# Row sums of four heads in one pass of the array, with their quotients spread through DRAM

## The chip, the cores and the metric

The kernel runs on one core of one Trainium2 chip. The metric is the time of one execution on the device in microseconds (us); lower is better. Runs of this kernel agree within about 0.02%: the three shown below lie between 2488.17 and 2488.77 us. The core has five engines that work side by side, each in its own order: TensorE (PE, with its weight loads PEld), VectorE (DVE), ScalarE (ACT), GpSimd (POOL) and SyncE (SP), which issues all DMA transfers here. Matmuls write to PSUM, the other engines read it; everything else lies in SBUF or in DRAM.

## The reference

Four layers work on x of shape (4, 512, 32, 32): four batches of 512 channels and 1024 tokens, all in fp32. Layers 0 and 3 are softmax attentions, layer 1 a linear attention, layer 2 a softmax attention with one head. The part that the change touches, from layer 0:

```python
attn = jnp.einsum('bihd,bjhd->bijh', q, k) * SCALE
attn = jax.nn.softmax(attn, axis=2)
res = jnp.einsum('bijh,bjhd->bihd', attn, v)
...
out = res @ Wo.T + bo + xs
```

Layer 0 has 8 heads of 64 channels, layer 3 has 4 heads of 128 and a group norm ahead of its projections. Softmax divides the exponentials of a row by their sum; the kernel divides after the product with v, which gives the same.

## The kernel before

The program has two paths. `plain_path` computes everything without subtracting the row's largest score and counts at the end whether all row sums and their reciprocals stayed below 1e18; `general_path` would run afterwards if they had not. With these inputs only `plain_path` runs, and only it is changed.

**Order.** TensorE runs its instructions in the order in which the program is written. The order on the other engines is settled when the kernel is built; each engine then executes its own list in order. Tiles come from pools with tags: a tag has so many buffers, and a new tile of the tag waits until the last reader of the old one is done.

**Layers.** Layer 0 goes over the four batches: projections of q, k and v for a batch, then its attention. While the projections of batch b run, layer 1 (linear attention) of batch b-1 is done piece by piece. Layer 2 follows for four batches (`one_head`), then layer 3. Large products use a seven-product scheme on 2x2 blocks, which is not touched.

**Attention of layers 0 and 3** (`attention`, L892). A unit is a query block `qb` (two of 512 queries) and a group `g` of 128 channels: four units to a query block, eight to a batch. In layer 0 a unit is a pair of heads of 64 (`pair`), in layer 3 one head of 128. Scores are computed with keys on the partitions and queries along the free axis. A step covers 128 keys in layer 0 (8 steps to a unit) and 256 in layer 3 (4 steps).

- `scores` (L908): the score products (L913 for pairs, in 64x64 quadrants of the array, or L918), the exponential on ACT into a tile `pt` (L922, four buffers), and on DVE the sum over steps into `acc` (L926, L929; tag `sum`, two buffers). In layer 3 the two halves of `acc` are added at the end (L931).
- `values` (L933): products of `pt` with v (L941 or L956) into PSUM accumulators of the tag `acc` (four buffers), two steps behind the scores. A pair uses two accumulators, added into the tile `ot` at the end of the unit (L951 on ACT, L952 on DVE). In layer 3 the one accumulator stays until the unit is normalised.
- `sum_rows` (L961): the sum over the partitions by a matmul with a matrix of ones, so that each of the 128 result rows holds the same row sum of its head. For a pair these are four quadrant products into two accumulators (L968), which ACT and DVE add (L973, L974); in layer 3 one full product (L976). `invert` (L673) then takes the reciprocal on DVE (L675, which is in the tile `rd`) and two DVE reductions, the largest sum and the largest reciprocal, for the range check (L677, L678).
- `normalise` (L980): `ot` times `rd` on DVE (L985), and on ACT the bias of the output projection added to x (L988).
- `project_out` (L996): the output projection of a query block in four parts, each of 256-column products (L1018) and DVE additions (L1026), the last ones into x. The first part needs groups 0 and 1 of `ot`, the second groups 2 and 3.

**Ticks.** Work that must wait is put in the list `later` with a number. Each step of values calls `tick` (L648), which counts all numbers down and runs what has come to zero. In layer 0 a unit's `sum_rows` and `normalise` come at tick 1 after it, in layer 3 the sum comes just ahead of the unit's last values. The four parts of `project_out` come at ticks 4, 5, 6, 7 after a query block in layer 0 and 2, 3, 3, 4 in layer 3.

**x.** A batch of x is 2 MB, 16 KB on each partition. The tag `x` has three buffers. `away` (L568) writes a batch to DRAM, `back` (L572) reads it again; both are issued by SP. In layer 2, while batch b is worked on, the layer norm of batch b+1 is prepared (`layer_norm`, L1466), and at the end of a batch it goes away and another one comes back.

Of the kernel before, what the change touches and what calls it, by code (L numbers as in the profile page):

```python
# [13 lines left out]
F32 = mybir.dt.float32  # L14
AF = mybir.ActivationFunctionType
ALU = mybir.AluOpType
AX = mybir.AxisListType

P = 128
# [455 lines left out]
def plain_path(ctx: ExitStack, tc: tile.TileContext, d: dict, out: bass.AP, count):  # L475
# [9 lines left out]


    nc = tc.nc
# [23 lines left out]
    def sum_tile(name):  # L511
        return work.tile([P, 2, TB], F32, tag="sum", bufs=2, name=name)

    def v_tiles():
# [49 lines left out]
    def x_tile(b):  # L564
        xs[b] = xpool.tile([P, NC, S], F32, tag="x", bufs=B - 1, name=f"x{b}")
        return xs[b]
# [24 lines left out]
    wo0 = load_wo(d["wo0"])  # L591
    for b in range(1, B - 1):
        nc.sync.dma_start(x_tile(b), xin[b])

# [22 lines left out]
    UNITS = B * NTB * (NC + 1 + NC)  # L617
    tops = const.tile([P, 2, UNITS], F32, name="tops")
    unit = itertools.count()

# [52 lines left out]
    def invert(rd, ps):  # L673

        nc.vector.reciprocal(rd, ps)  # L675
        n = next(unit)
        nc.vector.tensor_reduce(tops[:, 0, n : n + 1], ps, AX.X, ALU.max)  # L677
        closing[:] = [nc.vector.tensor_reduce(tops[:, 1, n : n + 1], rd, AX.X, ALU.max).ins]  # L678

# [212 lines left out]
    def attention(b, q, key, v, heads, scale, wo, os, bo, hooks={}, last=False, end=None, plain=False):  # L892
# [13 lines left out]
        half = lambda i: slice(i * P // 2, (i + 1) * P // 2)  # L906

        def scores(n):  # L908
            qb, g, i = steps[n]
# [12 lines left out]
            exps.append(nc.scalar.activation(pt, ps, AF.Exp, scale=scale).ins)  # L922
            pts[n] = pt
            if i == 1:
                accs[qb, g] = acc = sum_tile("sum")
                nc.vector.tensor_tensor(acc, pts[n - 1], pt, ALU.add)  # L926
            elif i > 1:
                acc = accs[qb, g]
                nc.vector.tensor_tensor(acc, acc, pt, ALU.add)  # L929
            if i == nsteps - 1 and not pair:  # L930
                nc.vector.tensor_tensor(acc[:, 0, :], acc[:, 0, :], acc[:, 1, :], ALU.add)  # L931

        def values(n):  # L933
# [20 lines left out]
            for s in range(2):  # L954
                j = 2 * i + s
                nc.tensor.matmul(  # L956
                    outs[qb, g][0], lhsT=v[j // 2][:, j % 2, bass.ts(g, P)], rhs=pt[:, s, :],
                    start=(j == 0), stop=(j == NT - 1),
                )

        def sum_rows(qb, g):  # L961
# [16 lines left out]
            invert(rds[qb, g], ps)  # L978

        def normalise(qb, g):  # L980
            rd = rds.pop((qb, g))
            if g == 0 and not pair:
                ots[qb] = chunks_tile("ot", "ot")
            o = ots[qb][:, g, :]
            nc.vector.tensor_tensor(o, o if pair else outs.pop((qb, g))[0], rd, ALU.mult)  # L985
            xv = x[:, g, bass.ts(qb, TB)]
            with tc.issue_after(exps[-1]):
                nc.scalar.activation(xv, xv, AF.Identity, bias=bo[:, g : g + 1])  # L988
# [108 lines left out]
        for m in range(0, len(steps) + 2, per):  # L1097
# [3 lines left out]
            for n in range(m, m + per):  # L1101
                if n >= 2:
                    qb, g, i = steps[n - 2]
                    final = i == nsteps - 1

                    if final and not pair:
                        sum_rows(qb, g)
                    values(n - 2)
                    tick()
                    if final and pair:  # L1110
                        later.append([1, lambda qb=qb, g=g: (sum_rows(qb, g), normalise(qb, g))])
                    elif final:
                        normalise(qb, g)
# [5 lines left out]
                    elif final and g == NC - 1:  # L1119
                        rest = []  # L1120
                        later.append(
                            [2 * per, lambda qb=qb, rest=rest: rest.extend(project_out(qb))]
                        )
                        for i in (1, 2, 3) if pair else (1, 1, 2):
                            later.append([2 * per + i, lambda rest=rest: rest.pop(0)()])
                if parts:
# [339 lines left out]
    def layer_norm(b, tb, tiles):  # L1466

        x = xs[b][:, :, bass.ts(tb, TB)]
        t = {}

        def add():
            s = t["s"] = row_tile("s")
            nc.vector.tensor_tensor(s, x[:, 0, :], x[:, 1, :], ALU.add)
            for c in range(2, NC):
                nc.vector.tensor_tensor(s, s, x[:, c, :], ALU.add)

        def center():
# [4 lines left out]
            for c in range(NC):  # L1482
                nc.vector.scalar_tensor_tensor(
                    xn[:, c, :], mean, -1.0 / C, x[:, c, :], ALU.mult, ALU.add
                )
# [76 lines left out]
    def verdict():  # L1562

        assert next(unit) == UNITS
        ok = const.tile([P, 2 * UNITS], F32, name="ok")
# [8 lines left out]
    with tc.manual_schedule(engines={mybir.EngineType.PE}):  # L1574
# [8 lines left out]
        for b in range(B):  # L1583
# [9 lines left out]
            if b > 0:  # L1593
                away(b - 1)
                if b == 1:
                    nc.sync.dma_start(x_tile(B - 1), xin[B - 1])
                else:
                    back(b - 2)
            if b == 0:
# [70 lines left out]
        for b in range(B):  # L1670
# [25 lines left out]
            if b == 0:  # L1696
                pieces.append(lambda: (away(B - 1), back(2)))
            parts = []
# [31 lines left out]
            away(b)  # L1730
            back((b + 3) % B)
            if b + 1 < B:
# [11 lines left out]
        for b in range(B):  # L1744
# [10 lines left out]
            flush()  # L1755
            if b == 1:
                xs.pop(0)
                back(B - 1)
            hooks = {}
# [77 lines left out]
```

## Time and profile before

| What | Value |
|---|---|
| Median of three runs | 2488.47 us (2488.17 to 2488.77) |
| The profiled execution | 2487.56 us |
| Its span, first to last instruction | 2485.8 us, 24942 instructions |
| Granted TensorE clock | 0.999 |
| Attention of layer 0, one batch (326.0 to 453.9) | 127.9 us, PE busy 126.95 |
| Attention of layer 3, one batch (1909.5 to 2038.8) | 129.3 us, PE busy 129.3 |
| Reciprocals L675 | 32 in layer 0, 3352 ns each; 32 in layer 3, 3357 ns each; 8 in layer 2 |
| Range reductions L677, L678 | 628 to 672 ns each |
| Exponentials L922 | 384, 1022 ns each |
| A batch of x to DRAM and back | 6.3 us and 7.8 us from issue to landing |

The profile is that of one execution. A line of a group reads: line of the kernel, engine, operation, what it writes and reads, shapes, number; then busy time in us, mean duration in ns; then the engine's idle time just before such instructions and what ended it. A line of the timeline starts with start and duration in us. `64*64` is the part of the array that a matmul uses, rows by columns. A matmul instruction in fp32 leaves two records, and the records of successive matmuls overlap, so that a busy TensorE is not yet a TensorE at its peak. The time from issue to landing of a DMA ends when all of it has arrived.

### The profile page before, as it was taken

The numbers are of one execution on the slowest core, as the hardware profiler recorded it, in microseconds if no ns is written. First come the engines' busy times: TensorE is split into PE (matmuls) and PEld (weight loads), VectorE is DVE, ScalarE is ACT, GpSimd is POOL, SyncE is SP. The second block draws the span as 40 slices with busy tenths as digits, with TensorE's granted clock in tenths as the row PEclk, the third lists the DMA queues.
The fourth block names the chain that finished last, engine by engine and source line by source line (L and its number), as shares of the span: only waits on it lengthen the run. The fifth ranks groups of instructions, "written<-read, shape, count | busy, mean of one in ns | idle before, by whom it ended". The sixth has DMA issues, their size and how long they took to land.

```text
span 2485.8 us, 24942 instructions
## 1 busy us (share of the span) xinstructions
PE 2468.6 (99%) x10218; PEld 1277.3 (51%) x10218; DVE 1679.0 (68%) x1941; ACT 705.0 (28%) x863; POOL 253.6 (10%) x240
## 2 busy tenths in 40 slices
PE   9999999999999999999999999999999999999999
PEld 4545544554455444544645546445556446555653
DVE  3788588858875888647486775755664773665465
ACT  1454154315531544221211201112211320321121
POOL 4001100110011001201203021021010001002000
PEclk9999999999999999999999999999999999999999
DMA  5000010001000301010101010110010000000000
GB/s 216 1 1 1 5 69 1 1 5 69 1 1 5 119 10 51 0 72 9 59 0 68 5 67 19 51 68 17 17 51 1 5 13 17 1 17 17 1 9 27
DMA packets 23304, 72.47 MB, mean 29 GB/s; under 512 B 1808, under 2 KB 9488, under 8 KB 21136
## 3 DMA queue, kind: packets, MB, share of 16 engines
q1 hardware_dynamic: 23184, 70.82, 7.8%
q8 instruction: 82, 1.34, 0.2%
q14 instruction: 38, 0.31, 0.0%
HBM read 44.60 MB, written 25.17 MB: 28 GB/s over the span
## 4 chain that ended last, share of the span: by engine, by line
PE 96%; DVE 3%; issue 1%; ACT 0%; DMA 0%; SPq 0%; DVEq 0%
PE acc L703 20%; PE acc L824 11%; PE sc L918 9%; PE acc L956 9%; PE sc L913 8%; PE acc L941 8%; PE acc L831 8%; PE acc L1018 6%; PE acc L1232 6%; PE acc L1193 2%; PE acc L968 1%; PE acc L976 1%; PE feat L638 1%; DVE sum L929 1%; PE acc L638 1%; DVE rd L675 1%
## 5 line engine op out<-in xcount | busy, mean ns | idle before, releaser
L922 ACT ACTIVATE pt<-sc 128x1024 f32<-128x1024 f32 x384 | 380.3, 1022 | 650.4 <-PE sc L918 391.5
L929 DVE TENSOR_TENSOR sum<-sum,pt 128x1024 f32<-128x1024 f32 x256 | 313.9, 1226 | 45.8 <-ACT pt L922 34.4
L941 PE MATMUL acc<-pt,v 64*64 64x512 f32 x2048 | 291.0, 590 | 0.0
L913 PE MATMUL sc<-q,k 64*64 64x512 f32 x2048 | 273.7, 591 | 1.1 <-ACT pt L922 1.1
L956 PE MATMUL acc<-pt,v 128*128 128x512 f32 x512 | 239.9, 592 | 0.0
L918 PE MATMUL sc<-q,k 128*128 128x512 f32 x512 | 239.8, 593 | 0.0
L675 DVE RECIPROCAL rd<-acc 128x512 f32<-128x512 f32 x32 | 107.4, 3357 | 107.0 <-PE acc L976 107.0
L691 POOL TENSOR_TENSOR ws<-wqkv 128x256 f32<-128x256 f32 (+1 forms) x40 | 40.6, 1015 | 1334.8 <-PE acc L968 552.3
L703 PE MATMUL acc<-t,ws 128*128 128x512 f32 x384 | 173.9, 593 | 0.0
L941 PEld LDWEIGHTS acc<-pt,v 64*64 64x64 f32 x2048 | 104.2, 133 | 121.3 <-issue 98.3
L913 PEld LDWEIGHTS sc<-q,k 64*64 64x64 f32 x2048 | 101.1, 133 | 123.6 <-issue 92.4
L956 PEld LDWEIGHTS acc<-pt,v 128*128 128x128 f32 x512 | 97.3, 190 | 122.5 <-issue 120.5
L918 PEld LDWEIGHTS sc<-q,k 128*128 128x128 f32 x512 | 96.8, 190 | 112.8 <-issue 88.1
L703 PEld LDWEIGHTS acc<-t,ws 128*128 128x128 f32 x384 | 72.5, 190 | 86.6 <-issue 85.1
L675 DVE RECIPROCAL rd<-rs 128x512 f32<-128x512 f32 x32 | 107.3, 3352 | 1.1
L926 DVE TENSOR_TENSOR sum<-pt 128x1024 f32<-128x1024 f32 x64 | 76.7, 1198 | 42.1 <-ACT pt L922 42.1
L742 ACT COPY v<-acc 128x512 f32<-128x512 f32 x24 | 14.0, 585 | 287.9 <-PE acc L824 287.9
L824 PE MATMUL acc<-ws,t 128*128 128x256 f32 x384 | 87.3, 379 | 0.0
L831 PE MATMUL acc<-qs,w 128*128 128x512 f32 x192 | 86.6, 593 | 0.0
L831 PE MATMUL acc<-q,ln 128*128 128x512 f32 x192 | 85.8, 593 | 0.0
L733 DVE TENSOR_TENSOR v<-acc,v 128x512 f32<-128x512 f32 x72 | 49.4, 688 | 51.9 <-PE acc L824 51.7
L742 ACT COPY q<-acc 128x512 f32<-128x512 f32 x40 | 23.4, 585 | 207.8 <-PE acc L703 207.8
(318 smaller groups left out, 3698.2 us busy)
## 6 DMA issues: line engine op xcount, KB each, us to landing
home<-x SPq DMA_DIRECT2D x8, 2048.0 KB, 6.3
x<-home SPq DMA_DIRECT2D x8, 2048.0 KB, 7.8
out<-x SPq DMA_DIRECT2D x32, 256.0 KB, 2.1
x<-in_x SPq DMA_DIRECT2D x3, 2048.0 KB, 16.9
wo<-in_wo SPq DMA_DIRECT2D x3, 1024.0 KB, 5.3
w<-in_w SPq DMA_DIRECT2D x1, 3072.0 KB, 17.8
wqkv<-in_wqkv SPq DMA_DIRECT2D x1, 3072.0 KB, 10.1
wqkv<-in_wqkv SPq DMA_DIRECT2D x2, 1024.0 KB, 9.2
```

The lines of the kernel that those rows point to most:

```text
L675: nc.vector.reciprocal(rd, ps)
L703: nc.tensor.matmul(ps, lhsT=w[:, m, :], rhs=x[:, m, :], start=start, stop=stop, skip_group_check=True)
L824: nc.tensor.matmul(ps[:, bass.ts(r, C // 2)], lhsT=x[:, m, bass.ts(2 * o + r, P)], rhs=w[:, m, :], start=(start and r == 0), stop=stop, sk ...
L831: nc.tensor.matmul(ps, lhsT=x[:, m, bass.ts(o, P)], rhs=w[:, m, :], start=start, stop=stop, skip_group_check=True,)
L913: nc.tensor.matmul(ps[half(h), s, :], lhsT=key(g, i)[half(s), half(h)], rhs=q[qb][half(s), g, :], start=True, stop=True,)
L918: nc.tensor.matmul(ps[:, s, :], lhsT=key(g, 2 * i + s), rhs=q[qb][:, g, :], start=True, stop=True)
L922: exps.append(nc.scalar.activation(pt, ps, AF.Exp, scale=scale).ins)
L929: nc.vector.tensor_tensor(acc, acc, pt, ALU.add)
L941: nc.tensor.matmul(outs[qb, g][r][half(s), :], lhsT=v[i // 2][half(r), i % 2, g * P + s * hd : g * P + (s + 1) * hd], rhs=pt[half(r), s, : ...
L956: nc.tensor.matmul(outs[qb, g][0], lhsT=v[j // 2][:, j % 2, bass.ts(g, P)], rhs=pt[:, s, :], start=(j == 0), stop=(j == NT - 1),)
L1018: nc.tensor.matmul(ps[i][:, bass.ts(o, n)], lhsT=w[:, m, bass.ts(o, P)], rhs=t[:, m, :], start=(start and m + o == 0), stop=(stop and m == ...
L1232: nc.tensor.matmul(ps[i, o], lhsT=w[m][:, bass.ts(o, P)], rhs=t[m], start=(start and m == 0), stop=(stop and m == 3), skip_group_check=True,)
```

## The change

Four parts, all in `plain_path`:

- **Shared row sums.** Units are put together in groups: in layer 0 two units (four heads), three groups to a batch, with the last two units of a batch left alone; in layer 3 the four units of the first query block and the first three of the second, with the last unit left alone. `sum_shared` does one product for each head of a group, with 32 columns of ones, into 32 partitions of one accumulator. One reciprocal then serves the whole group. To make room, the sums of a unit are kept until its group closes in a new tile `many`.
- **Quotients through DRAM.** One row of each head's reciprocals is written to DRAM and read back onto all partitions of its head, into a new tile `rds`, by two transfers in layer 0 and one in layer 3. The units of the group are normalised after that, in layer 3 from `ot`, to which ACT copies the values at the end of each unit. The parts of `project_out` of the first query block come one tick later in layer 0 (5, 6, 7, 8) and two ticks later in layer 3 (4, 5, 5, 6); after the second they come when they did.
- **Range check on ACT.** `invert` no longer reduces to the largest values on DVE. Two ACT activations sum the row sums and the reciprocals into the same table; their other output overwrites the row sums.
- **Two batches of x on chip.** The tag `x` gets two buffers in place of three, which gives the room for `many` and `rds`. Each batch is loaded or read back one step later.

```diff
+    def many_tile(name):
+        return work.tile([P, NC, TB], F32, tag="many", name=name)
...
-        xs[b] = xpool.tile([P, NC, S], F32, tag="x", bufs=B - 1, name=f"x{b}")
+        xs[b] = xpool.tile([P, NC, S], F32, tag="x", bufs=2, name=f"x{b}")
...
     def invert(rd, ps):
 
-        nc.vector.reciprocal(rd, ps)
-        n = next(unit)
-        nc.vector.tensor_reduce(tops[:, 0, n : n + 1], ps, AX.X, ALU.max)
-        closing[:] = [nc.vector.tensor_reduce(tops[:, 1, n : n + 1], rd, AX.X, ALU.max).ins]
+        closing[:] = [nc.vector.reciprocal(rd, ps).ins]
+        n, m = next(unit), rd.shape[0]
+        for i, t in enumerate((ps, rd)):
+            nc.scalar.activation(ps, t, AF.Identity, accum_out=tops[:m, i, n : n + 1])
...
+        if pair:
+            shared = [[(qb, g), (qb, g + 1)] for qb in range(NTB) for g in range(0, NC, 2)][:-1]
+        else:
+            shared = [[(qb, g) for g in range(NC - qb)] for qb in range(NTB)]
...
             if i == 1:
-                accs[qb, g] = acc = sum_tile("sum")
+                acc = many_tile("sum")[:, :2, :] if pair and g % 2 and us else sum_tile("sum")
+                accs[qb, g] = acc
...
             if i == nsteps - 1 and not pair:
-                nc.vector.tensor_tensor(acc[:, 0, :], acc[:, 0, :], acc[:, 1, :], ALU.add)
+                total = acc[:, 0, :]
+                if us:
+                    if g == 0:
+                        parts_of[qb] = many_tile("sums")
+                    total = accs[qb, g] = parts_of[qb][:, g, :]
+                nc.vector.tensor_tensor(total, acc[:, 0, :], acc[:, 1, :], ALU.add)
...
+            if i == nsteps - 1:
+                if g == 0:
+                    ots[qb] = chunks_tile("ot", "ot")
+                if (qb, g) in group_of:
+                    nc.scalar.copy(ots[qb][:, g, :], outs.pop((qb, g))[0])
...
+        def sum_shared(us):
+
+            heads = [(u, s) for u in us for s in range(2 if pair else 1)]
+            n = P // 4
+            ps = acc_tile()
+            for k, (u, s) in enumerate(heads):
+                acc = accs[u]
+                nc.tensor.matmul(
+                    ps[k * n : (k + 1) * n, :], lhsT=ones[:, :n],
+                    rhs=acc[:, s, :] if pair else acc, start=True, stop=True,
+                )
+            m = len(heads) * n
+            rd = row_tile("rd")
+            invert(rd[:m], ps[:m])
+            spread = work.tile([P, NC, TB], F32, tag="rds", name="rds")
+
+            home = dram.tile(
+                [len(heads), TB], F32, tag=f"quotients{len(heads)}", bufs=2, name="quotients"
+            )
+            nc.sync.dma_start(home, rd[0:m:n])
+            for s in range(2 if pair else 1):
+                to = spread[half(s) if pair else slice(0, P)]
+                nc.sync.dma_start(
+                    to[:, : len(us), :],
+                    home[s :: 2 if pair else 1].partition_broadcast(to.shape[0]),
+                )
...
-                    if final and not pair:
+                    us = group_of.get((qb, g))
+                    closes = us and (qb, g) == us[-1]
+                    if final and not pair and closes:
+                        sum_shared(us)
+                    elif final and not pair and not us:
                         sum_rows(qb, g)
                     values(n - 2)
                     tick()
-                    if final and pair:
+                    if final and pair and closes:
+                        later.append(
+                            [1, lambda us=us: [normalise(*u) for u in sum_shared(us)]]
+                        )
...
+                        lead, *others = (4, 5, 6, 7) if pair else (2, 3, 3, 4)
+
+                        wait = (1 if pair else 2) if us else 0
                         later.append(
-                            [2 * per, lambda qb=qb, rest=rest: rest.extend(project_out(qb))]
+                            [lead + wait, lambda qb=qb, rest=rest: rest.extend(project_out(qb))]
                         )
...
-                if b == 1:
-                    nc.sync.dma_start(x_tile(B - 1), xin[B - 1])
+                if b + 1 < B:
+                    nc.sync.dma_start(x_tile(b + 1), xin[b + 1])
                 else:
-                    back(b - 2)
+                    back(0)
...
-                pieces.append(lambda: (away(B - 1), back(2)))
+                pieces.append(lambda: (away(B - 1), back(1)))
...
             away(b)
-            back((b + 3) % B)
+            back((b + 2) % B)
...
-            if b == 1:
-                xs.pop(0)
-                back(B - 1)
+            if 0 < b < B - 1:
+                xs.pop(b - 1)
+                back(b + 1)
```

## The prediction

> **What bounds the kernel now.** I read the page's first part, then the chain of waits.
>
> ```profile
> PE 2468.6 (99%) x10218; PEld 1277.3 (51%) x10218; DVE 1679.0 (68%) x1941; ACT 705.0 (28%) x863; POOL 253.6 (10%) x240
> PE 96%; DVE 3%; issue 1%; ACT 0%; DMA 0%; SPq 0%; DVEq 0%
> ```
>
> TensorE sets the time in every stage: only matmuls taken away, or TensorE waits made, can move it. Next, the groups with shapes kept apart and the busy time by stretch (one attention of layer 0, one of layer 3).
>
> ```profile
> L968 PE MATMUL acc<-sum,ones 64*64 64x512 f32 x256 | 47.5, 604 | 1.3 <-DVE ot L952 1.2
> L976 PE MATMUL acc<-sum,ones 128*128 128x512 f32 x64 | 32.7, 592 | 0.0
> core 0: us, PE busy (x) PEld busy (x) DVE busy (x) ACT busy (x) POOL busy (x), PEclk, DMA share, GB/s
> 326.00:453.90 127.90, 126.95 (x1094) 58.42 (x1098) 114.07 (x107) 73.14 (x84) 3.89 (x4) 1.00 0.06 24
> 1909.50:2038.80 129.30, 129.30 (x334) 62.78 (x333) 85.09 (x96) 41.06 (x44) 4.47 (x7) 1.00 0.03 8
> ```
>
> A matmul instruction leaves two records: 32 pair units with 4 instructions make 256 records, 32 units of layer 3 with one make 64. A record's length overlaps the next, so I go by starts. In the timeline a full 512-column instruction takes 0.858 us (8 records in 3.43), and four quadrant instructions together take the same: the sums at 342.41 are followed by the values at 343.27. DVE is 89% busy in layer 0's attention, ACT 57%; in layer 3 both have room.
>
> **Sums removed.** Layer 0: 6 of 8 units in each of 4 batches lose a 0.858 us sum, 24 units. Layer 3: 7 of 8, 28 units. 52 x 0.858 = -44.6 us.
>
> **Sums added.** Layer 0 gets 3 groups a batch, layer 3 two: 20 groups. If their 32-column instructions run side by side, a group costs 0.858: +17.2. No row shows 128x32; the nearest shows two 128x64 instructions abreast:
>
> ```profile
> 284.19 0.14 PEld L1370 LDWEIGHTS acc<-v,kf 128*64 128x64 f32 x2 [0.28 <-issue]
> 284.62 0.14 PEld L1370 LDWEIGHTS acc<-v,kf 128*64 128x64 f32 x2 [0.29 <-issue]
> ```
>
> Two weight loads go in every 0.43 us, where the full array takes one. Bounds: 0.858 a group (four abreast, as 64x64 runs), and no overlap, 12 x 3.43 + 4 x 3.43 + 4 x 2.57 = 65.2; two abreast 34.3. I take 17.2, because both nearby shapes fill the array.
> The Trainium skill (TensorE: Matmul & The Clock Gate, "Measured speedup vs the span model") gives 2.38x for three column tiles at 512 columns. By that share of the ideal, an estimate from that page, a group would cost about 1.08 us and the term be 21.6; no trace here shows it.
>
> **Array shape changed and changed back.** The timeline around the first output projection of batch 1:
>
> ```profile
> 386.92 0.68 DVE L952 TENSOR_TENSOR ot<-ot,acc 128x512 f32<-128x512 f32 x1
> 387.65 0.65 PE L968 MATMUL acc<-sum,ones 64*64 64x512 f32 x3 [0.21 <-DVE ot L952]
> 390.69 3.35 DVE L675 RECIPROCAL rd<-rs 128x512 f32<-128x512 f32 x1
> 392.96 1.99 PE L1018 MATMUL acc<-ot,wo 128*128 128x256 f32 x8
> 394.88 1.95 PE L913 MATMUL sc<-q,k 64*64 64x512 f32 x16
> 395.09 0.68 DVE L985 TENSOR_TENSOR ot<-ot,rd 128x512 f32<-128x512 f32 x1
> 396.65 1.04 PE L941 MATMUL acc<-pt,v 64*64 64x512 f32 x8
> 397.62 1.99 PE L1018 MATMUL acc<-ot,wo 128*128 128x256 f32 x8
> ```
>
> Before, the product at 395.09 was done ahead of the second part at 397.62: no wait. Eight 256-column records need 1.72 us, so from 392.96 to 394.88 the change to 64x64 costs 0.20; back, 396.65 + 0.86 to 397.62, 0.11. With 0.15 after the 128x64 stretches I take 0.33 a group: 20 x 0.33 = +6.6, bounds 0 and 20 x 0.8 = 16 (the longest issue gaps of the weight loads are 0.8).
> The Trainium skill (TensorEngine Tiling (Array Packing), "Key Properties") speaks against the change here: switching the tiling mode drains the array. It gives no price; without it the sum would be 6.6 lower.
>
> **Waits for an accumulator that go.** At 387.65 the old sum waited for the addition at 386.92, since it needs two of four accumulators beside the two of the running unit. The list of waits has:
>
> ```profile
> PEld acc L968 <- DVE ot L952: 11.4, 12, 1.4
> ```
>
> The shared sum needs one. From the matmul starts, the 64x64 stretch of a batch before this projection takes 2.27 us more than its records need, 2.28, 2.27 and 2.62 in the others; less the switch, about 2.05 x 4 = -8.2 (bounds -12 and 0).
>
> **The way through DRAM.** Before, the quotient is ready 3.35 us after the row sum is in SBUF. Now a write of 8 KB and broadcast reads follow: two of 256 KB in layer 0, one of 1 MB in layer 3. Rows for these:
>
> ```profile
> out<-x SPq DMA_DIRECT2D x32, 256.0 KB, 2.1
> wo<-in_wo SPq DMA_DIRECT2D x3, 1024.0 KB, 5.3
> DMA to landing us min/median/max: 3.1/3.2/3.3
> ```
>
> (The last is two broadcast loads of 256 KB each, issued 0.4 apart, tile brows.) Layer 0, counted from the end F of unit (0,3)'s values. TensorE: two scores 1.72, values 0.86, sum 1.2 with its switches, so the sum ends at F+3.8. DVE, with additions in the way, starts the reciprocal at F+5.5 and ends at F+9. Write to F+11.1, reads 3.7 with the second's issue, F+14.8; two products at 0.6 pitch, seen by TensorE at F+16.3. The second part of the projection, now at tick 6, would start at F+13.8 (ticks 2 to 5: 0.86, 2.57, 0.86, 2.57; first part 2.0 with switches; values 0.86; switch 0.2). It waits 2.5 us, four times: +10. Bounds: 0 (a reciprocal that starts at once and products that come first) and 24 (3.5 us more each, one more queue of DVE additions).
> Behind the waiting second part stand the next scores on TensorE, so the exponentials too. On DVE the products wait ahead of the additions L929, and their lateness would hold the four pt buffers; DVE loses 3 reciprocals, 16 range reductions and 6 additions a batch (24 of its 114 us), which covers the 2 to 3 us. SP has only transfers of x beside these in attention.
> Layer 3: from the sum's start S, reciprocal S+1.1 to S+4.4, write to S+6.5, read 5.3 to S+11.8, four products to S+14.5, the first two by S+13.2. The first part's tick comes at S+2.9+4 x 3.43 = S+16.6. Nothing waits: 0. The other groups have a whole unit (14.6 us) between their close and the first reader, and the units that keep the old way have no transfer.
> The single tile ot is late next: the second query block's first copy into it must now wait for the last part of the projection, which stands behind it on TensorE (tick 8, layer 3 tick 6). Two accumulators stay held until then; the next values need two, freed by DVE additions about 1 us after that part, and two scores (1.72) lie between. I leave it at 0, bound 1 us in 8 places.
>
> **Range check and copies on ACT.** Per check two 128x512 activations of 0.72 (row L988) and 0.19 to read the accumulator (row L1333): 1.8 us, 5 checks a batch in layer 0, 9 us there against 3.5 of row-sum copies gone; layer 3 adds 9.5 with its seven copies. Both fit the idle share. But ACT executes in order, and the first activation overwrites what the reciprocal reads: an exponential queued behind it can wait up to 3.35 us. In layer 0 an exponential has about 1.3 us to spare (ends 347.17, its score buffer is wanted at 348.4); layer 3 has about 4. So between 0 and 20 checks x 2 = 40 us; I take +3, since a check queued where its operand is ready waits little. Layer 2's 8 checks fall where ACT is nearly idle: 0.
>
> **Two batches of x.** The loads are the same, only later. Layer 2 now needs x2 right after the load issued at 1185.35 that lands at 1193.2; the first TensorE consumer is at 1207.57. x1 lands at 1101.8, wanted at 1116.5; x0 at 1495.4, and its statistics run from 1496.6 anyway. 0 to 6 us, I take +1. If the cover went, each load would cost its lateness against those times.
>
> **Sum:** -44.6 + 17.2 + 6.6 - 8.2 + 10 + 3 + 1 = -15.0 us. The profiled execution is 2487.56 us (span 2485.8, 1.8 around it), 0.9 below the median 2488.47: 2472.6 and 2473.5. I say 2474. Range of this case: 2462 to 2486 (the wait from 0 to 20, the check from 0 to 5).
>
> **Rivals.**
> Transfer hidden: no wait in the second part and none on ACT, -28 us, 2459. For it: DVE is lighter by a fifth. Against: the 2.5 us count.
> Slower, one mechanism: checks queued on ACT ahead of exponentials in layer 0. Price 2 us x 20 = 40 instead of 3: 2473.5 + 37 = 2510. It decides from 0.9 us a check (18 us, which eats the gain). For it: the order is fixed before the run, and the reciprocal takes 3.35 us where other DVE work of that size takes 0.68. Against: before, ACT hardly ever waits for DVE in attention (2.4 us in all).
> Longer round trip: 6 us more each, +24, 2497; for it, the write must land before the reads; against, the landings above.
> No gain from columns: two abreast 2473.5 + 17.1 = 2491, none abreast 2522; the 128x64 row is against both.
>
> **How the numbers follow.** Forecast 0.55, hidden 0.12, ACT 0.13, round trip 0.12, columns 0.08. About 0.2% (5 us) is what a measurement here tells from no change. Faster, under 2483.5: nearly all of the forecast (0.51) and the hidden case, 0.63. Same: edges of the forecast, mild round trips and two-abreast columns, 0.15. Slower: 0.22. The range reaches from the hidden case less 3, 2456, to 2500, past the round trip; most of the ACT case and no overlap stay outside.
>
> **What would show it.** Groups 128x32 at about 0.86 us between neighbours with 0.3 of switching; sums of 128x128 gone but for four; DVE's idle time before its products ended by the spread transfer; TensorE's weight loads at L1018 waiting about 2.5 us for these products, four times; no ACT wait for a reciprocal over 1 us ahead of an exponential. Wrong it is if four columns take more than one pass, if exponentials stand behind the check, or if weight loads in layer 2 wait for x.

## The result: a little slower

The changed kernel takes 2496.74 us (2495.12 to 2498.38), the kernel before 2488.32 in the same comparison: a ratio of 1.0034, 95% interval 1.0023 to 1.0045, or 8.4 us slower. The forecast was 2474 and faster: the time lies in the range given (2456 to 2500), the sign is wrong. The profiled execution took 2496.46 us (span 2494.7, clock 0.998).

The page's busy times and the chain of waits, of the changed kernel:

```profile
PE 2450.4 (98%) x10122; PEld 1224.3 (49%) x10122; DVE 1487.5 (60%) x1742; ACT 756.5 (30%) x1027; POOL 251.1 (10%) x240
PE 92%; DVE 4%; ACT 2%; issue 1%; DMA 0%; SPq 0%; DVEq 0%; ACTq 0%
```

TensorE's records sum to 18.2 us less than before (2468.6), so matmuls did go. But its share of the chain falls from 96% to 92%: DVE and ACT now stand between matmuls, where ACT had 0%. The busy time by stretch, for the same two stretches as before (one attention of layer 0, one of layer 3; columns as before):

```profile
332.39:466.08 133.69, 126.14 (x1068) 47.61 (x1072) 96.78 (x87) 73.96 (x94) 3.60 (x4) 0.99 0.11 35
1929.36:2055.03 125.67, 125.67 (x334) 60.27 (x333) 60.78 (x72) 47.55 (x59) 4.47 (x6) 1.00 0.07 24
```

Layer 3 became 3.63 us shorter (129.30 to 125.67), with TensorE always busy. Layer 0 became 5.8 longer (127.90 to 133.69) while TensorE's busy time fell by 0.8 and DVE's by 17: idle time, 7.55 us of it in one batch. Over the program, by the starts of the same matmuls in both traces: layer 0 +22.4 for its four batches, layer 2 -0.4, layer 3 -14.3, and 1.3 from the first loads; together +9.0 at the end; the two profiled executions differ by 8.9.

A smaller part of layer 0 is the clock and not a wait. In two stretches of the changed kernel, in the second and the fourth batch, the granted clock (third column from the end) was half:

```profile
447.20:450.60 3.40, 3.40 (x20) 1.07 (x16) 1.31 (x2) 1.51 (x2) 0.00 (x0) 0.50 0.55 137
966.00:969.40 3.40, 3.40 (x20) 1.07 (x16) 3.37 (x5) 2.78 (x5) 0.00 (x0) 0.51 0.02 5
```

Sixteen records of values that take 1.71 us at full clock take 2.92 in the first of them (448.23 to 451.15). Each stretch costs about 1.7 us, so the two make 3.4 of the 22.4; the trace of the kernel before has none in layer 0.

The list of waits, of the changed kernel (engine, tile, line, what ended the wait; us in total, times, longest):

```profile
PEld sc L923 <- ACT pt L932: 67.4, 48, 3.1
ACT acc L680 <- DVE rd L677: 57.7, 21, 6.5
DVE ot L1037 <- DMA rds<-quotients: 27.3, 12, 3.8
```

The same wait of the scores' weight loads for the exponential was 8.6 us in the kernel before:

```profile
PEld sc L913 <- ACT pt L922: 8.6, 12, 1.2
```

The second and third lines of the changed kernel are new: the range check's activation on ACT waits for the reciprocal, and the products on DVE wait for the spread quotients. The timeline of the changed kernel around the first shared sum of batch 1 shows how the first two belong together:

```profile
362.64 1.06 PE L1009 MATMUL acc<-sum,ones 128*32 128x512 f32 x8
363.64 1.09 PE L958 MATMUL acc<-pt,v 64*64 64x512 f32 x8
364.55 1.90 PE L923 MATMUL sc<-q,k 64*64 64x512 f32 x16
364.59 3.35 DVE L677 RECIPROCAL rd<-acc 128x512 f32<-128x512 f32 x1
...
366.26 1.90 PE L958 MATMUL acc<-pt,v 64*64 64x512 f32 x16
...
368.04 0.58 ACT L680 ACTIVATE acc<-acc 128x512 f32<-128x512 f32 x1 [3.82 <-DVE rd L677]
...
368.62 1.01 ACT L932 ACTIVATE pt<-sc 128x1024 f32<-128x1024 f32 x1
369.53 0.60 ACT L680 ACTIVATE acc<-rd 128x512 f32<-128x512 f32 x1
...
369.69 1.09 PE L923 MATMUL sc<-q,k 64*64 64x512 f32 x8 [1.53 <-ACT pt L932]
...
371.21 1.09 PE L923 MATMUL sc<-q,k 64*64 64x512 f32 x8 [0.43 <-ACT pt L932]
```

ACT stands for 3.82 us at L680, until the reciprocal has ended at 367.94. The exponentials for the scores of 364.55 stand behind it, although their operands are there. TensorE still has its values at 366.26 (16 records, 1.72 us, to 367.98), then no free score buffer until 369.69, and after eight records (0.86 us) none again until 371.21: 1.71 and 0.66, 2.4 us for one group. (The weight loads go ahead of the matmuls, so their waits in the list above come out longer.) That is the rival "checks queued on ACT ahead of exponentials". The shared sum itself costs what was forecast: its eight records at 362.64 are followed by values one microsecond later, the change of shape included.

Further on in the same batch, at the first output projection, of the changed kernel:

```profile
404.14 1.99 PE L1070 MATMUL acc<-ot,wo 128*128 128x256 f32 x8
405.55 1.29 DVE L1037 TENSOR_TENSOR ot<-ot,rds 128x512 f32<-128x512 f32 x2 [2.08 <-DMA rds<-quotients]
...
406.06 1.09 PE L958 MATMUL acc<-pt,v 64*64 64x512 f32 x8
...
407.08 1.99 PE L1070 MATMUL acc<-ot,wo 128*128 128x256 f32 x8
```

The second part, at 407.08, does not wait for the products, though DVE waited for the transfer. TensorE had lost so much by then that the transfer was in time. One wait hides another here, so what each costs can't be read from this trace alone.

### The profile page after: what moved, and what is told of

Same layout as the page of the kernel before. It is cut to its first block, busy times and chain, and to the rows that moved or that the text cites. A ratio compares the mean times of both kernels' runs of the same rounds, so it can differ in the third digit from the quotient of the medians.

```text
span 2494.7 us, 24739 instructions
## 1 busy us (share of the span) xinstructions
PE 2450.4 (98%) x10122; PEld 1224.3 (49%) x10122; DVE 1487.5 (60%) x1742; ACT 756.5 (30%) x1027; POOL 251.1 (10%) x240
## 4 chain that ended last, share of the span: by engine, by line
PE 92%; DVE 4%; ACT 2%; issue 1%; DMA 0%; SPq 0%; DVEq 0%; ACTq 0%
PE acc L705 20%; PE acc L826 11%; PE acc L973 9%; PE sc L928 9%; PE acc L833 8%; PE acc L1070 7%; PE sc L923 7%; PE acc L958 7%; PE acc L1298 6%; DVE rd L677 2%; PE acc L1259 2%; ACT pt L932 2%; DVE sum L941 2%; PE feat L640 1%; PE acc L640 1%
## 5 line engine op out<-in xcount | busy, mean ns | idle before, releaser
L941 DVE TENSOR_TENSOR sum<-sum,pt 128x1024 f32<-128x1024 f32 x256 | 314.3, 1228 | 184.6 <-ACT pt L932 176.0
L923 PE MATMUL sc<-q,k 64*64 64x512 f32 x2048 | 252.8, 596 | 32.6 <-ACT pt L932 32.6
L958 PE MATMUL acc<-pt,v 64*64 64x512 f32 x2048 | 253.3, 596 | 0.0
L923 PEld LDWEIGHTS sc<-q,k 64*64 64x64 f32 x2048 | 75.6, 133 | 181.5 <-issue 112.1
L958 PEld LDWEIGHTS acc<-pt,v 64*64 64x64 f32 x2048 | 79.3, 134 | 143.7 <-issue 138.9
L677 DVE RECIPROCAL rd<-acc 128x512 f32<-128x512 f32 (+1 forms) x24 | 80.4, 3352 | 39.2 <-PE acc L1009 39.2
L1070 PE MATMUL acc<-ot,wo 128*128 128x256 f32 x336 | 80.6, 383 | 0.0
L826 PEld LDWEIGHTS acc<-ws,t 128*128 128x128 f32 x384 | 73.0, 190 | 11.2 <-issue 1.4
```

Of the source, the lines that this page charges most:

```text
L677: closing[:] = [nc.vector.reciprocal(rd, ps).ins]
L826: nc.tensor.matmul(ps[:, bass.ts(r, C // 2)], lhsT=x[:, m, bass.ts(2 * o + r, P)], rhs=w[:, m, :], start=(start and r == 0), stop=stop, sk ...
L923: nc.tensor.matmul(ps[half(h), s, :], lhsT=key(g, i)[half(s), half(h)], rhs=q[qb][half(s), g, :], start=True, stop=True,)
L958: nc.tensor.matmul(outs[qb, g][r][half(s), :], lhsT=v[i // 2][half(r), i % 2, g * P + s * hd : g * P + (s + 1) * hd], rhs=pt[half(r), s, : ...
L1070: nc.tensor.matmul(ps[i][:, bass.ts(o, n)], lhsT=w[:, m, bass.ts(o, P)], rhs=t[:, m, :], start=(start and m + o == 0), stop=(stop and m == ...
```

## The experiments

All ratios are against the kernel before (about 2488.4 us in every comparison), with 95% intervals. Diffs are against the changed kernel unless another is named.

### The check back on DVE

```diff
-        closing[:] = [nc.vector.reciprocal(rd, ps).ins]
+        nc.vector.reciprocal(rd, ps)
         n, m = next(unit), rd.shape[0]
-        for i, t in enumerate((ps, rd)):
-            nc.scalar.activation(ps, t, AF.Identity, accum_out=tops[:m, i, n : n + 1])
+        nc.vector.tensor_reduce(tops[:m, 0, n : n + 1], ps, AX.X, ALU.max)
+        closing[:] = [nc.vector.tensor_reduce(tops[:m, 1, n : n + 1], rd, AX.X, ALU.max).ins]
```

> The changed kernel with the range check back on DVE as two reductions; nothing else differs. Theory A (the check stands on ACT ahead of exponentials and waits there for the reciprocal, so TensorE waits for scores' buffers in layer 0): the 9 us a batch of waits go, 37 us in all, and up to 2.5 us a batch of waiting for the quotients may appear in their place: 2460 to 2470 us, layer 3 unchanged. Rival B (the way through DRAM is what costs, and ACT's wait lies over it): waits of TensorE move to the output projection, 2488 or more. Rival C (two batches of x): 2494 to 2497, nothing moves.

Measured: 2482.83 us (2481.70 to 2485.86), ratio 0.9979 (0.9969 to 0.9989). The sign turns, but only 13.9 us come back, and none of the expectations holds. What lies under the check shows in this kernel's timeline of the first projection:

```profile
391.32 3.35 DVE L677 RECIPROCAL rd<-acc 128x512 f32<-128x512 f32 x1
...
394.69 0.53 SPq L1021 DMA_DIRECT2D quotients<-rd  x1
...
396.46 1.24 SPq L1024 DMA_DIRECT2D rds<-quotients  x2
...
397.39 1.99 PE L1070 MATMUL acc<-ot,wo 128*128 128x256 f32 x8
...
401.54 1.29 DVE L1037 TENSOR_TENSOR ot<-ot,rds 128x512 f32<-128x512 f32 x2 [3.28 <-DMA rds<-quotients]
...
402.38 1.97 PE L1070 MATMUL acc<-ot,wo 128*128 128x256 f32 x8 [1.98 <-DVE ot L1037]
```

From the end of the reciprocal (394.67) to the first product (401.54) the way through DRAM takes 6.87 us, and the second part of the projection now waits for it, 1.7 to 2.2 us in the four batches: the 2.5 of the prediction. But the first shared sum of a batch, where no projection is near, has a cost too; the same kernel's timeline:

```profile
371.85 1.29 DVE L1037 TENSOR_TENSOR ot<-ot,rds 128x512 f32<-128x512 f32 x2 [2.88 <-DMA rds<-quotients]
...
373.06 1.22 DVE L941 TENSOR_TENSOR sum<-sum,pt 128x1024 f32<-128x1024 f32 x1
...
374.37 1.03 ACT L932 ACTIVATE pt<-sc 128x1024 f32<-128x1024 f32 x1 [1.28 <-DVE sum L941]
...
377.19 1.09 PE L923 MATMUL sc<-q,k 64*64 64x512 f32 x8 [0.43 <-ACT pt L932]
```

DVE stands 2.88 us in front of a product that nobody needs yet. The additions L941 behind it are late, so the `pt` buffers stay taken, so the exponential waits 1.28 us, so scores come late. It is the same pattern as on ACT, one engine further on. After the third group it costs more: TensorE is idle 1.56 and 0.76 us (to 450.41 and 452.05 in batch 1) at the old sum of the unit left alone, which needs the late additions too.

### The check on ACT alone, in the kernel before

The row sums stay as they were; only `invert` gets the two activations (and `tops` a memset). Against the kernel before:

```diff
-        nc.vector.reciprocal(rd, ps)
-        n = next(unit)
-        nc.vector.tensor_reduce(tops[:, 0, n : n + 1], ps, AX.X, ALU.max)
-        closing[:] = [nc.vector.tensor_reduce(tops[:, 1, n : n + 1], rd, AX.X, ALU.max).ins]
+        closing[:] = [nc.vector.reciprocal(rd, ps).ins]
+        n, m = next(unit), rd.shape[0]
+        for i, t in enumerate((ps, rd)):
+            nc.scalar.activation(ps, t, AF.Identity, accum_out=tops[:m, i, n : n + 1])
```

> The kernel before with the range check alone moved to ACT. Theory A: 32 checks in layer 0 at about 1.5 to 2.4 us each, 48 to 77 us: 2535 to 2565 us, all of it in layer 0, layers 2 and 3 within 3 us of before. Rival B (the way through DRAM costs): within 5 us of before, 2484 to 2493.

Measured: 2519.21 us (2518.74 to 2519.95), ratio 1.0123 (1.0106 to 1.0140), +30.8. The time lies between the two expectations: the mechanism stands by itself, at about half the price that the first one set. By the starts of the stages layer 0 loses 7.9 us a batch, 0.99 for each of its 32 checks, and layers 2 and 3 lose nothing. The list of waits of this kernel (layer 0's check is `rs`, layer 3's `acc`):

```profile
ACT acc L679 <- DVE rd L676: 89.4, 29, 6.0
ACT rs L679 <- DVE rd L676: 68.7, 32, 2.6
```

ACT waits longer in layer 3, 3.1 us each, and it costs nothing there; in layer 0 it waits 2.1 and this costs 1. The length of a wait doesn't tell its price; what stands behind it and how much time that has does.

### Two batches of x alone

Against the kernel before, the core of it:

```diff
-        xs[b] = xpool.tile([P, NC, S], F32, tag="x", bufs=B - 1, name=f"x{b}")
+        xs[b] = xpool.tile([P, NC, S], F32, tag="x", bufs=2, name=f"x{b}")
...
-            back((b + 3) % B)
+            back((b + 2) % B)
```

> The kernel before with two batches of x on chip and their later loads, nothing else. Theory A: all loads land ahead of their readers, 2488 to 2490 us. Rival C (the later loads cost): 2492 or more, with waits in layer 2.

Measured: 2487.43 us (2486.61 to 2488.55), ratio 0.9995 (0.9986 to 1.0005). It costs nothing.

### The same activations, later in ACT's order

```diff
-    def invert(rd, ps):
+    def invert(rd, ps, late=0, exps=None):
...
-        for i, t in enumerate((ps, rd)):
-            nc.scalar.activation(ps, t, AF.Identity, accum_out=tops[:m, i, n : n + 1])
...
+        def check(after=None):
+            with tc.issue_after(after) if after is not None else nullcontext():
+                for i, t in enumerate((ps, rd)):
+                    nc.scalar.activation(ps, t, AF.Identity, accum_out=tops[:m, i, n : n + 1])
...
+        if late:
+            later.insert(0, [late, lambda: check(exps[-1])])
+        else:
+            check()
...
-            invert(rd[:m], ps[:m])
+            invert(rd[:m], ps[:m], 3 if pair else 1, exps)
```

> The changed kernel with the same two activations of the check on ACT, but queued behind the exponentials that are issued up to three ticks after the sum (one tick in layer 3); only the check of a batch's last unit stays where it was. Theory A (the place in ACT's order costs, not the work): 2462 to 2475 us. Rival D (ACT's work costs: 1.8 us a check where exponentials have little to spare): 2490 to 2497.

Measured: 2484.26 us (2480.61 to 2487.48), ratio 0.9984 (0.9974 to 0.9993). ACT does all its work and the time is that of the kernel with the check on DVE (0.9979), within the intervals. So with the trip in place the check costs by its place, not by its work; without the trip this wasn't run. The time expected of it was too low, because the wait for the transfer lay under it here too.

### Layer 0 without the way through DRAM

Against the kernel with the check on DVE:

```diff
             invert(rd[:m], ps[:m])
+            if pair:
+                for u in us:
+                    accs.pop(u)
+                    rds[u] = rd
+                return us
```

> The changed kernel with the check on DVE, and in layer 0 without the way through DRAM: the products take the reciprocals as they lie, 32 rows to a head, so layer 0's quotients are not those of the reference (left out: the write and both reads). Theory A2 (what is left in layer 0 is DVE standing at the products until the reads land, three times a batch, and TensorE behind it; from the trace with the check on DVE 1.1 us after the first group, 2.2 at the projection, 2.2 after the third, 22 us in all): 2459 to 2466 us. Rival E (the rest lies in the 32-column sums, their switches or the later parts of the projection): 2478 or more.

Measured: 2454.99 us (2454.73 to 2455.11), ratio 0.9866 (0.9850 to 0.9883), 27.8 us less than with the trip and 4 under the range of A2. Layer 0's way through DRAM costs 27.8 us and not 10. Each batch of layer 0 is now 4.9 us shorter than before the change, each of layer 3 3.63 as in the changed kernel.

### The check on ACT without the trip

The same lines put into the changed kernel itself, with the check on ACT at its old place.

> The changed kernel with the range check on ACT, as it was changed, but without the way through DRAM in layer 0 (the products there take the reciprocals as they lie; layer 0's quotients are not the reference's). With the kernel without both (2455.0), the one with the trip alone (2482.8) and the changed kernel (2496.5) it makes a table of four. G, the two waits lie over each other: the check alone costs what the idle time of the changed kernel's trace gives, about 2.4 us at three groups and 1.9 us at the unit alone, 9 us a batch, so 2455 + 36 = 2491 (2480 to 2496). H, the two waits add: the check costs 13.9 us with or without the trip, 2469 (2464 to 2474).

Measured: 2490.25 us (2489.82 to 2491.83), ratio 1.0009 (1.0000 to 1.0019). G holds. The timeline of this kernel at the first shared sum of batch 1:

```profile
364.92 1.90 PE L958 MATMUL acc<-pt,v 64*64 64x512 f32 x16
366.63 1.29 DVE L1042 TENSOR_TENSOR ot<-ot,rd 128x512 f32<-128x512 f32 x2
366.69 0.58 ACT L680 ACTIVATE acc<-acc 128x512 f32<-128x512 f32 x1 [3.82 <-DVE rd L677]
...
368.34 1.09 PE L923 MATMUL sc<-q,k 64*64 64x512 f32 x8 [1.53 <-ACT pt L932]
```

The products follow the reciprocal at once and DVE waits for no transfer, yet ACT's 3.82 and TensorE's idle 1.7 are the same as in the changed kernel. The busy time over the attention of this batch:

```profile
331.04:463.03 131.99, 124.44 (x1068) 47.14 (x1072) 97.63 (x87) 73.96 (x94) 3.60 (x4) 1.00 0.06 23
```

The changed kernel has as many records of TensorE in its stretch and takes 1.70 us more (133.69), all of it busy time (126.14): the half clock. The idle time is 7.55 us in both, so in this batch the trip adds no wait to those of the check. The four kernels together, in us:

| | no trip in layer 0 | trip |
|---|---|---|
| check on DVE | 2454.99 | 2482.83 |
| check on ACT | 2490.25 | 2496.74 |

The check costs 35.3 alone, the trip 27.8 alone, both 41.75, not 63.1. Undoing only the check shows 13.9 of its 35.3, undoing only the trip 6.5 of its 27.8.

Part of the trip's price is the clock. The profile with the check on DVE has two stretches at half clock, from 204.0 and from 698.9; the batches that hold them take 136.68 and 136.41 us from their first scores to the next stage, the other two 134.92 and 134.61. The two kernels without the trip have none. So some 3.5 of the 27.8 us are clock, and some 3.4 of the 6.5. The mean granted clock was 0.995 to 0.999 in the 38 runs of the four kernels that make layer 0's trip with the products right behind it (the changed one, the check on DVE, the check later, one group fewer) and 0.999 or 1.000 in all others. The lower clock goes with these kernels, then; why it falls no run here shows.

### Products later

Against the kernel with the check on DVE: the products of a batch's first and third group are issued six ticks after the sum, behind the DVE additions written by then.

```diff
+        def products(us):
+            with tc.issue_after(adds[-1]):
+                for u in us:
+                    normalise(*u)
...
-                        later.append([1, lambda us=us: [normalise(*u) for u in sum_shared(us)]])
+                        if us[-1] == (0, NC - 1):
+                            later.append([1, lambda us=us: [normalise(*u) for u in sum_shared(us)]])
+                        else:
+                            later.append([1, lambda us=us: sum_shared(us)])
+                            later.append([7, lambda us=us: products(us)])
```

> The changed kernel with the check on DVE, and the products of the first and third group of a batch in layer 0 issued six ticks after the sum, behind the additions of the scores issued until then; the second group as it was. Theory A2: the 3.3 us a batch after the first and third group go and the 2.2 at the projection stay: 2468 to 2473 us. Rival F (DVE's standing still costs nothing, only the projection's wait does): 2480 to 2484.

Measured: 2465.87 us (2465.42 to 2467.64), ratio 0.9910 (0.9893 to 0.9926). That is 2 us under the range of A2. 17.0 of the trip's 27.8 us go with the place of these products: mostly DVE standing in front of products that had no reader yet, and some 3.5 us of clock, which is 1.000 in this kernel's runs but for the profiled one (0.999, one stretch at half clock, 1.6 to 2.2 us slower than the others). The 10.9 us left over the kernel without the trip are mostly at the projection, where this trace still has 1.8 to 2.1 us of waiting in a batch.

### Products and projection later

Against the one before: the second group's products too, at tick 5, and the parts of the first projection at 5, 7, 7, 8 in layer 0 instead of 5, 6, 7, 8.

```diff
-                        if us[-1] == (0, NC - 1):
...
+                        later.append([1, lambda us=us: sum_shared(us)])
+                        late = 5 if us[-1] == (0, NC - 1) else 7
+                        later.append([late, lambda us=us: products(us)])
...
-                        lead, *others = (4, 5, 6, 7) if pair else (2, 3, 3, 4)
+                        lead, *others = ((4, 6, 6, 7) if us else (4, 5, 6, 7)) if pair else (2, 3, 3, 4)
```

> As with the later products of the first and third group, and besides the second group's products behind the additions issued until tick 5 and the second and third part of the projection both at tick 7 in layer 0. Theory A2: both costs go but some 0.7 us of waiting for accumulators between the parts: 2461 to 2468 us. Rival E: 2478 or more.

Measured: 2457.07 us (2455.86 to 2458.61), ratio 0.9877 (0.9860 to 0.9893): 31.3 us faster than the kernel before, the best that computes everything, 2.1 above the one without the trip, and 4 under the range of A2. Its timeline at the first projection of batch 1, and its busy time over the attention of that batch:

```profile
388.28 1.99 PE L1075 MATMUL acc<-ot,wo 128*128 128x256 f32 x8
...
392.50 1.29 DVE L1042 TENSOR_TENSOR ot<-ot,rds 128x512 f32<-128x512 f32 x2 [0.70 <-DMA rds<-quotients]
392.83 1.04 PE L963 MATMUL acc<-pt,v 64*64 64x512 f32 x8
393.80 1.99 PE L1075 MATMUL acc<-ot,wo 128*128 128x256 f32 x8
```

```profile
321.38:445.11 123.73, 123.62 (x1070) 48.16 (x1074) 98.49 (x92) 68.94 (x78) 3.84 (x4) 1.00 0.12 38
```

The products end at 393.79, just as the second part starts at 393.80 with no wait shown; between the two parts lie a step's values, scores and values instead of values alone. By its records TensorE is idle 0.11 us in the stretch, where the changed kernel had 7.55.

### That kernel with the check on ACT

`invert` as in the changed kernel, all else as just shown.

> The kernel whose products and projection of layer 0 come later (2457.1 with the check on DVE), with the check on ACT as it was changed. Here the trip waits for nobody any more, but is made. G: the check's price shows in full, 2457 + 36 = 2493 (2482 to 2498). H: 2471 (2466 to 2476).

Measured: 2488.38 us (2487.47 to 2488.98), ratio 1.0000 (0.9991 to 1.0010). The trip is made and hidden, and the check costs 31.3 us, 89% of what it costs without a trip. It alone eats the whole gain.

### One group fewer in layer 0

Against the kernel with the check on DVE: units 2 and 3 of the first query block are summed alone, so no trip ends at the first projection.

```diff
-            shared = [[(qb, g), (qb, g + 1)] for qb in range(NTB) for g in range(0, NC, 2)][:-1]
+            shared = [[(qb, g), (qb, g + 1)] for qb in range(NTB) for g in (0,)]
```

> The changed kernel with the check on DVE, and units (0,2) and (0,3) of layer 0 summed alone as before, so that the projection waits for no transfer (it comes at its old ticks). Theory A2: the 2.2 us at the projection go, one sum (0.86) comes back less a switch (0.25), and up to 1 us of waiting for accumulators: -1.6 to -0.6 us a batch, 2476 to 2481 us. Rival F: -9, 2474 or less.

Measured: 2490.54 us (2487.72 to 2493.96), ratio 1.0009 (1.0000 to 1.0019): 7.7 us slower than with the group, which neither theory expected. Its profile has three stretches at half clock, one more than with the group, some 1.7 us of the 7.7. The timeline of this kernel at the first unit summed alone:

```profile
371.52 1.29 DVE L1037 TENSOR_TENSOR ot<-ot,rds 128x512 f32<-128x512 f32 x2 [2.99 <-DMA rds<-quotients]
...
375.84 1.04 PE L990 MATMUL acc<-sum,ones 64*64 64x512 f32 x2 [1.23 <-DVE sum L941]
...
376.74 0.68 DVE L969 TENSOR_TENSOR ot<-ot,acc 128x512 f32<-128x512 f32 x1
377.34 2.54 DVE L941 TENSOR_TENSOR sum<-sum,pt 128x1024 f32<-128x1024 f32 x2
377.48 1.13 PE L990 MATMUL acc<-sum,ones 64*64 64x512 f32 x3 [0.60 <-DVE ot L969]
```

The old sum needs the last addition of its unit and two accumulators, which DVE frees at L969. Both are late because DVE stood 2.99 us at the products of the group ahead of it, until 371.52. F looked only at the projection; here a sum of the old kind right after a shared group loses more to the late DVE than the group that it replaced. So the waits that the change takes away (old sums) and those that it makes (products) are not independent either.

## Why the prediction was wrong, step by step

**The step that failed** is the range check on ACT, taken at +3 "since a check queued where its operand is ready waits little". It is queued where its operand is not ready: right after the sum, 3.35 us ahead of the end of the reciprocal. It measures 35.3 us without the trip, 31.3 with the trip hidden, all of it in layer 0. The price was in the text: the rival said 2 us a check, decided from 0.9. TensorE's idle time in the run with the check and no trip is 2.43 us at each of a batch's three groups, 1.89 at the first of its two lone units, 0 at the last, which closes the batch: 9.2 a batch, 36.7 in all, against the 40 that the rival set for 20 checks. Layer 3's cost nothing, as the 4 us of room there said. The argument against it, that ACT hardly ever waited for DVE before, came from an order in which no ACT instruction read a reciprocal, so it said nothing on where a new one would be put.

**The way through DRAM**, +10, was sized at the wrong places. At the projection it was right: 1.7 to 2.2 us a batch against 2.5, and 8.8 us went from the run with products later to the one with the projection later too. The trip itself took 6.87 us against 5.8 summed from rows. But that what DVE loses ("24 of its 114 us") "covers the 2 to 3 us" was wrong: 17.0 us, some 3.5 of them clock, go with DVE waiting in order in front of products, at groups that the prediction called free since they have a whole unit before the first reader. Less work over the batch didn't help at that place: DVE stood 2.88 us there, and an exponential behind its next addition waited 1.28.

**The sum of both** went by plus signs, and they don't add: 35.3 + 27.8 cost 41.75 together. That the time fell into the range given is luck for this reason: added, the two prices make 2518, outside it.

**What was right.** Layer 3: 7 sums less and 2 groups more are 5 x 0.858 = 4.29 a batch, less two switches of 0.33: 3.63. The traces give 3.63, its trip covered. Four 32-column products do run side by side: the eight records of a group start within 0.48 us, the second four 0.45 after the first, and the next product starts 1.00 us after the group, change of shape included. With 0.858 for the group the switches around it in layer 0 are 0.11 and 0.14, 0.25 against 0.33. By the prediction's estimate from the lower speed-up that the Trainium skill has for three column tiles (TensorE: Matmul & The Clock Gate, "Measured speedup vs the span model") a group would take 1.08 us, 0.54 from the first four records to the second four; the measured 0.45 decides for 0.858. Its rule that a change of the tiling mode drains the array (TensorEngine Tiling (Array Packing), "Key Properties") agrees in kind, at that quarter of a microsecond. The two batches of x cost nothing (-0.9, inside the interval) against +1. The waits that go were under-sized: in the kernel without the trip a batch of layer 0 is 4.86 us shorter, of which the sums give 2.57 and the switches take 0.75, so 3.0 of waiting went, against 2.05. One place of it is a part of the projection that started 0.96 us late before and 0.11 there; the rest was not put down to places.

In measured terms: the kernel with the check on DVE and no trip in layer 0 stands at -33.4 us (2454.99 to 2488.4; the prediction's terms for that are -44.6 + 17.2 + 6.6 - 8.2 + 1 = -28.0), then +35.3 + 27.8 - 21.4 for their overlap = +8.3, against the measured 8.4. The overlap is taken from the same four times, so that this sum closes proves nothing more.

What stays open: a check on ACT placed later was run only together with the trip in its early form, not in the fastest kernel; the 2.1 us that this kernel has above the one without the trip were not searched for; and why the clock falls is not known.

## What to carry to other kernels

On engines that run in order, an instruction that waits for something late costs by what stands behind it, not by its own length: with the trip in place the same activations cost 14 us in one place and nothing measurable a few exponentials later, and products issued behind additions that were ready won 17 us, some 3.5 of it clock. So when a change adds an operand that comes late (a slow reciprocal, a transfer), place its reader where the operand is there, even if nothing else seems to want the engine. Two such waits in one stretch can hide each other, as here: undo both, and each without the other, before pricing either.

## What the runs showed of the hardware

Matmuls with 32 columns of 128 rows ran four abreast: four instructions of 512 columns in fp32 and the change of shape behind them take 1.00 us together (362.64 to 363.64), where one full instruction takes 0.858. The list of that line, of the changed kernel (records, their durations in ns, forms):

```profile
L1009 PE MATMUL acc<-sum,ones x96: 592/605/617, 112.4 to 940.3; 128*32 128x512 f32 x96
```

Sending 8 KB to DRAM and reading it back onto all partitions took long for its size, in the kernel with the check on DVE: 1.70 us from the write's issue at 394.69 until it has landed (396.39), the reads of 256 KB issued at 396.46 and 397.09 landing at 400.37 and 401.44, so 3.9 and 4.4 us each.

The granted clock can fall to 0.50 for about 3.4 us in the middle of a kernel whose mean is 0.998. Of the profiles here it does so, ahead of the last microseconds, only where layer 0 makes the trip: twice in the changed kernel, with the check on DVE and with the check later, three times with one group fewer, once with the products later, and not with products and projection later (check on DVE or on ACT).
